# A decoder layer on one core: products of distances 3 and 4 made during attention, three score buffers, eight transposes, moments of the norms on ScalarE

## The chip, the cores and the metric

The kernel runs on one core of a Trainium2 chip, in one launch. The metric is the device time of that launch in microseconds (us), and lower is better. The core has a matrix engine (TensorE, "PE" in the profile, with its weight loads as "PEld"), three engines for work on elements (VectorE "DVE", ScalarE "ACT", GpSimd "POOL") and SyncE ("SP"), which in this kernel issues all the transfers between the device memory and the on-chip memory. TensorE writes into accumulators in PSUM. Each engine takes its instructions strictly in the order of its own queue, and waits on semaphores for what the others produce.

## The reference

The layer has three parts, each followed by a residual sum and a layer norm. There are 16 sequences of 256 tokens with 512 features.

```
x = layernorm(x + attention(x))         # 16 heads of 32, causal, BitLinear weights:
                                        # ternary weights, activations rounded to 8 bits
x = layernorm(x + xattn(ctx, ctx, x))   # 32 heads of 8 features, along the feature axis L = 512
x = layernorm(x + ffn(x))               # rms norm with gamma, BitLinear 512 -> 512
```

The second part is, for each head, with k = v = ctx and q = x:

```
kv  = einsum('bhil,bhjl->bijhl', k_, v_)          # all products of two of the 8 features
y   = causal convolution of kv with ssm_kernel    # along l, 512 taps a head
out = y + kv * D
out = einsum('bijhl,bhil->bjhl', out, q_)
```

Since k and v are the same, kv(i, j) equals kv(j, i), so that 36 of the 64 products are enough. The kernel orders them by the distance d = j - i. With the features wrapped around (feature 8 is feature 0 again) distances 0 to 3 have 8 products each and distance 4 has 4.

## The kernel before

**Attention (first part of the time, up to about 429 us).** The 16 sequences run through a pipeline written out by hand: `step(b)` lists for every engine the stages of sequences b-2 to b+3 in the order in which they are issued, and `last_step` does so for the last three. For each sequence there are four groups of four heads. `scan` makes scores and takes their maxima (L341, L346). `weigh(b, g)` makes the scores again, transposed (L374, L381), takes the exponential on ScalarE into a tile p (L386), zeroes what lies above the diagonal with two selects on GpSimd (L390), and adds two of p's parts into `both` there (L396). `values(b, g)` multiplies p with the values (L409) and sums p and `both` (L416) on TensorE. The tiles p and low come from the pool `hp` with three buffers. Further stages divide by the sums (`divide_sums`, `divide`), round the result (L182, L188), turn it by a transfer (`turn_out`, L473), multiply it with the output weights (`close`, L482), take the norm's statistics (`moments`, `normalize`), and turn the normed rows into x1t (`keep`, L528, L529). `lay` (L355 to L358) splits the maxima for the next sequence. SP's queue holds, in a step, the input rows (L233), the residual rows (L425) and the transfers that transpose (`turn_out` L473, `turn_in` L279).

**The heads (from about 430 us).** 32 heads follow each other. For head h, `load` issues three transfers: the context c (L745), its first four features once more (L746), and the taps w (L749), each into one of three buffers. The products kv, a tile of 576 columns for each of four blocks of 128 positions, are made from c by `square` on ScalarE for distance 0 (L760), and by `multiply(k)` on GpSimd (L754): distance 1, then distance 2 together with distance 4, then distance 3. `copy` brings the head's x1t as q (L772, L773) on ScalarE. `block(lb)` convolves on TensorE: output block lb needs lb + 1 products of a 128 x 128 matrix of taps with kv, in two halves of 288 columns (L785), into a tile y of two PSUM banks, of which there are two buffers. VectorE then multiplies y with q in five operations (L797, L800, L803, L809, L812) into `own` and `turn`. `add` sums on GpSimd: own + turn (L960), and for blocks 1, 2 and 3 (FOLDED) it folds the four parts into two (L962). `read` transposes these parts with TensorE and sums them in PSUM (L820), two transposes for a folded block and four for block 0, so ten for a head, into the tile tok (two buffers). The last head's block 3 is read without adding (`read_all`, L975).

From tok on, the norm and the feed-forward part follow. `second_moments` takes mean and variance on VectorE (L835, L837), and writes a quarter of variance plus epsilon (L840) for one or two forms. `engine_roots` takes the square root on ScalarE (L845), `newton` betters it (L851 on VectorE, L855 on ScalarE), `inverse_roots` inverts (L863). `second_centred` and `second_max` (L878, L882) and the small operations of `second_norm` give the scales; ScalarE makes x2 (L888) and the rounded row (L897, L188), `turn` transposes it by a transfer (L902), `feed_product` multiplies it with the weights on TensorE (L907), `feed_forward` makes r3 (L911) and its statistics on VectorE by the same `moments2`, and `finish` norms it (L926) and stores it (L927). The loop at L1072 gives the order: in its turn h, the blocks of head h stand between the reads and the norm of head h-1, the feed-forward product of head h-2 and the store of head h-3. `last_heads` writes the end out.

Of the kernel before, what the change touches and what calls it, by code (L numbers as in the profile page):

```python
# [15 lines left out]
P = 128  # L16
# [16 lines left out]
def decoder_kernel(ctx: ExitStack, tc: tile.TileContext, x, ctx_t, w_q, w_k, w_v, w_o, ker, d_skip, gamma, w_f, out):  # L33
# [8 lines left out]
    taps = taps_pool.tile([XH, E + P], F32, name="taps")  # L42

# [174 lines left out]
    hp = att.enter_context(tc.tile_pool(name="hp", bufs=3, side="right"))  # L218
# [314 lines left out]

    def on(stage, b, *more):
        if 0 <= b < B:
            stage(batches[b], *more)

    def step(b):


        on(scan, b + 1, 0)
        on(lay_turned, b, b)
        on(fetch_x, b + 3, b + 3)
        on(fetch_again, b - 1, b - 1)
        on(values, b - 1, NB - 1)
        on(begin_batch, b + 2)
        scale = project_qk(batches[b + 2], 0, (0,), wait=True) if b + 2 < B else None
        on(spread, b + 2, b + 2)
        on(save_sums, b - 1)
        on(moments, b - 2)  # L550
        if scale:
            scale()
        on(weigh, b, 0)
        if b < 2:
            weight_round(3 + b, 0)
        if b == 0:
            weight_size(4, nc.scalar)
        on(project_qk, b + 2, 1)
        on(normalize, b - 2)
        on(divide_sums, b - 1)  # L560
        on(divide, b - 1, 0)

        on(scan, b + 1, 1)
        on(divide, b - 1, 1)
        on(out_scales, b - 1)
        on(values, b, 0)
        on(weigh, b, 1)
        if b == 0:
            weight_scale(4, weight_total(ps, 4))
        if b < 2:  # L570
            weight_round(3 + b, 1)
            weight_store(3 + b, 0)
        on(project_qk, b + 2, 2)
        on(out_scaled, b - 1)
        on(keep, b - 2, b - 2)

        on(scan, b + 1, 2)
        on(fetch_scales, b + 3, b + 3)
        on(out_rounded, b - 1)
        on(turn_out, b - 1)  # L580
        on(project_v, b + 2, 0)
        on(values, b, 1)
        on(values_scale, b + 3)
        on(fetch_scaled, b + 3, b + 3)
        on(weigh, b, 2)
        on(project_v, b + 2, 1)
        on(project_qk, b + 2, 0, (1,))
        if b < 2:
            weight_store(3 + b, 1)

        on(scan, b + 1, 3)
        on(project_qk, b + 2, 3)
        on(lay, b + 1, b + 1)
        on(fetch_rounded, b + 3)
        on(turn_in, b + 3, b + 3)
        on(values, b, 2)
        on(weigh, b, 3)
        on(close, b - 1)

    def last_step():  # L600
# [6 lines left out]
        fetch_again(n, B - 2)  # L607
        values(n, NB - 1)
        save_sums(n)
        weigh(m, 1)  # L610
        normalize(k)
# [117 lines left out]
    with ExitStack() as l2:  # L729
        lp = l2.enter_context(tc.tile_pool(name="lp", bufs=3, side="right"))  # L730
        cp = l2.enter_context(tc.tile_pool(name="cp", bufs=2, side="right"))
        ps_y = l2.enter_context(tc.tile_pool(name="ps_y", bufs=2, space=PSUM, side="right"))
        pb = l2.enter_context(tc.tile_pool(name="pb", bufs=1, side="right"))
        gam = pb.tile([P, E], F32, name="gam")
        op = l2.enter_context(tc.tile_pool(name="op", bufs=5, side="right"))
# [5 lines left out]
        def prepare(h):  # L741
# [22 lines left out]
            def multiply(k):  # L764
                part(k * P, XD, 0, k)
                if k == 2:
                    part(4 * P, 4, 0, 4)

# [6 lines left out]
            return w, kv, q, multiply, copy, square  # L775

        FOLDED = (1, 2, 3)
        Y0 = E - HALF

        def products(lb, w, kv):  # L780
            y = ps_y.tile([P, 2 * E], F32, name="y")
# [51 lines left out]
        def moments2(src, roots, forms):  # L833
            st = sm.tile([P, 6], F32, name="st2")
            nc.vector.bn_stats(st, src)  # L835
            mv = sm.tile([P, 2], F32, name="mv2")
            nc.vector.bn_aggr(mv, st)  # L837
            for i in forms:
                a, b = FORMS[i]
                nc.vector.tensor_scalar(roots.quarter[:, i : i + 1], mv[:, 1:2], a / 4, b / 4, ALU.mult, ALU.add)  # L840
            return mv[:, 0:1]
# [23 lines left out]
        def shifted(mean, res):  # L865
            shift = sm.tile([P, 1], F32, name="shift")
            nc.vector.tensor_scalar(shift, mean, res, -1.0, ALU.mult, ALU.mult)
            return shift
# [7 lines left out]
        def second_centred(m):  # L876
            m.xn = fp.tile([P, E], F32, name="xn")
            nc.vector.scalar_tensor_tensor(m.xn, m.flat, m.mean, gam, ALU.subtract, ALU.mult)  # L878
# [65 lines left out]

        def copy(m, *blocks):
            m.inputs[4](*blocks)
# [40 lines left out]
        def last_heads(three):  # L987
# [3 lines left out]
            read(last, 0)  # L991
            read(last, 2)
# [28 lines left out]
        with tc.manual_schedule(engines=by_hand):  # L1021
# [42 lines left out]
            ps_k = l2.enter_context(tc.tile_pool(name="ps_k", bufs=2, space=PSUM))  # L1064
            ps2 = l2.enter_context(tc.tile_pool(name="ps2", bufs=2, space=PSUM))
# [6 lines left out]
            for h in range(XH):  # L1072
# [5 lines left out]
                on(read, h - 1, 0)  # L1078
                on(read, h - 1, 2)
                on(multiply, h + 1, 1)  # L1080
                on(square, h + 1)

                on(block, h, 1)
# [7 lines left out]
                if h > 0:  # L1091
                    newton(roots)
# [3 lines left out]
                on(feed_product, h - 2)  # L1096
                if h > 0:
# [6 lines left out]
                on(copy, h + 1)  # L1104
                on(feed_forward, h - 2, ahead)
# [3 lines left out]
                on(read, h, 1)  # L1109
# [38 lines left out]
```

## Time and profile before

| | us |
|---|---|
| median of three runs | 853.55 (853.28 to 854.99) |
| the profiled execution, whole time | 852.3 |
| the profiled execution, its span | 850.6 |
| busy, share of the span: PE | 793.9 (93%) |
| PEld | 558.9 (66%) |
| DVE | 688.3 (81%) |
| ACT | 426.9 (50%) |
| POOL | 583.5 (69%) |

The span is cut into 40 slices below; each digit is the busy share of a slice in tenths (9 is 90% or more), and PEclk is the clock that TensorE was granted, in tenths.

```profile
PE   4889999999999999998768999999999999999993
PEld 3556666666666666665546777777777777777772
DVE  6757887787897778877556889888988898889885
ACT  6455655656655555664553344344434443344434
POOL 5265454554545545544638999999999999999980
PEclk9999999999999999999989999999999999999997
```

The two parts can be seen in POOL's row: half busy in attention, nearly always busy from slice 23 on. Times that name a moment are us from the start of the span. A row of the timeline gives start, length, engine, line, operation, tiles and shapes, and in brackets the idle time before it with what ended it. A row of the chain of waits gives start, length and what it was; "issue" is time in which nothing is seen to be waited for.

### The profile page before, as it was taken

The numbers are of one execution on the slowest core, as the hardware profiler recorded it, in microseconds if no ns is written. First come the engines' busy times: TensorE is split into PE (matmuls) and PEld (weight loads), VectorE is DVE, ScalarE is ACT, GpSimd is POOL, SyncE is SP. The second block draws the span as 40 slices with busy tenths as digits, with TensorE's granted clock in tenths as the row PEclk, the third lists the DMA queues.
The fourth block names the chain that finished last, engine by engine and source line by source line (L and its number), as shares of the span: only waits on it lengthen the run. The fifth ranks groups of instructions, "written<-read, shape, count | busy, mean of one in ns | idle before, by whom it ended". The sixth has DMA issues, their size and how long they took to land.

```text
span 850.6 us, 20122 instructions
## 1 busy us (share of the span) xinstructions
PE 793.9 (93%) x7678; PEld 558.9 (66%) x7754; DVE 688.3 (81%) x1889; ACT 426.9 (50%) x707; POOL 583.5 (69%) x652
## 2 busy tenths in 40 slices
PE   4889999999999999998768999999999999999993
PEld 3556666666666666665546777777777777777772
DVE  6757887787897778877556889888988898889885
ACT  6455655656655555664553344344434443344434
POOL 5265454554545545544638999999999999999980
PEclk9999999999999999999989999999999999999997
DMA  9112323332222222120240232433233333332311
GB/s 316 51 23 61 70 64 76 76 77 39 51 70 70 76 77 55 42 48 23 66 122 13 76 89 66 94 100 92 69 88 100 94 73 83 99 95 73 81 38 56
DMA packets 102207, 64.51 MB, mean 76 GB/s; under 512 B 66464, under 2 KB 83104, under 8 KB 102112
## 3 DMA queue, kind: packets, MB, share of 16 engines
q1 hardware_dynamic: 102112, 63.23, 28.3%
q8 instruction: 61, 1.00, 0.5%
q14 instruction: 34, 0.28, 0.1%
HBM read 43.34 MB, written 8.47 MB: 61 GB/s over the span
## 4 chain that ended last, share of the span: by engine, by line
PE 80%; DVE 7%; ACT 6%; issue 4%; POOL 3%; DMA 0%; ACTq 0%; POOLq 0%; DVEq 0%
PE y L785 34%; PE s L341 6%; PE acc L293 6%; PE s L381 6%; PE tok L820 5%; ACT p L386 4%; PE pv L409 4%; PE s L334 4%; DVE nmax L346 3%; PE acc_o L482 3%; PE acc_f L907 3%; PE sums L416 2%; PE s L374 2%; PE acc_v L311 2%; PE tp L528 1%
## 5 line engine op out<-in xcount | busy, mean ns | idle before, releaser
L785 PE MATMUL y<-kv,w 128*128 128x288 f32 x1280 | 334.8, 409 | 0.3 <-POOL kv L754 0.3
L785 PEld LDWEIGHTS y<-kv,w 128*128 128x128 f32 x1280 | 236.0, 190 | 60.7 <-POOL kv L754 0.8
L390 POOL TENSOR_SCALAR_AFFINE_SELECT p<-p 128x512 f32<-128x512 f32 x128 | 81.3, 659 | 139.5 <-ACT p L386 129.1
L960 POOL TENSOR_TENSOR own<-own,turn 128x512 f32<-128x512 f32 x127 | 162.0, 1275 | 12.1 <-DVE turn L812 9.9
L754 POOL TENSOR_TENSOR kv<-c 128x512 f32<-128x512 f32 (+1 forms) x128 | 144.4, 1140 | 2.9 <-PE sums L416 2.9
L346 DVE TENSOR_REDUCE nmax<-s 128x4 f32<-128x512 f32 (+1 forms) x128 | 116.5, 952 | 35.4 <-PE s L341 35.4
L386 ACT ACTIVATE p<-s 128x1536 f32<-128x1536 f32 x64 | 92.9, 1452 | 70.3 <-PE s L381 70.2
L396 POOL TENSOR_TENSOR both<-p 128x512 f32<-128x512 f32 x64 | 82.3, 1286 | 5.3
L845 ACT ACTIVATE root<-quarter 128x3 f32<-128x3 f32 (+2 forms) x34 | 7.0, 205 | 150.4 <-DVE quarter L840 150.4
L962 POOL TENSOR_TENSOR own<-own 128x256 f32<-128x256 f32 x95 | 69.1, 727 | 7.4
L797 DVE SCALAR_TENSOR_TENSOR own<-y,q 128x128 f32<-128x128 f32 x128 | 36.7, 286 | 43.7 <-PE y L785 35.7
L293 PE MATMUL acc<-xit,w 128*128 128x256 bf16 x504 | 68.9, 276 | 3.1 <-DVE w L158 2.9
L803 DVE TENSOR_TENSOR turn<-y,q 128x384 f32<-128x384 f32 x128 | 70.2, 548 | 0.0
L800 DVE TENSOR_TENSOR own<-y,q 128x384 f32<-128x384 f32 x128 | 70.1, 548 | 0.0
L293 PEld LDWEIGHTS <-w 128*128 128x128 bf16 x512 | 46.0, 100 | 23.9 <-issue 8.5
L341 PE MATMUL s<-kt,qt 32*128 32x128 f32 (+1 forms) x1024 | 60.0, 348 | 0.0
L820 PE MATMUL tok<-ident,own 128*128 128x128 f32 x318 | 57.7, 283 | 1.7 <-POOL own L962 1.5
L820 PEld LDWEIGHTS tok<-ident,own 128*128 128x128 f32 x318 | 37.8, 141 | 30.0 <-POOL own L962 20.1
L381 PE MATMUL s<-qt,kt 32*128 32x256 f32 (+1 forms) x1024 | 57.4, 335 | 0.0
L409 PE MATMUL pv<-p,va 128*32 128x256 f32 (+1 forms) x1024 | 54.9, 332 | 0.0
L421 ACT COPY ot<-pv 128x256 f32<-128x256 f32 x64 | 23.9, 373 | 50.8 <-PE pv L409 50.2
L334 PE MATMUL s<-mask,ident_h 128*128 128x256 bf16 x256 | 38.3, 272 | 11.1 <-ACT p L386 9.9
(148 smaller groups left out, 1348.4 us busy)
## 6 DMA issues: line engine op xcount, KB each, us to landing
xt<-in_x SPq DMA_DIRECT2D x16, 512.0 KB, 4.6
xr<-in_x SPq DMA_DIRECT2D x16, 512.0 KB, 5.2
c<-in_ctx_t SPq DMA_DIRECT2D x32, 256.0 KB, 3.3
w<-taps SPq DMA_DIRECT2D x32, 256.0 KB, 4.2
out_y<-res SPq DMA_DIRECT2D x31, 256.0 KB, 2.3
c<-in_ctx_t SPq DMA_DIRECT2D x32, 128.0 KB, 3.3
x1t<-in_w_q SPq DMA_DIRECT2D x1, 1024.0 KB, 6.4
x1t<-in_w_k SPq DMA_DIRECT2D x1, 1024.0 KB, 9.7
```

The lines of the kernel that those rows point to most:

```text
L293: nc.tensor.matmul(acc[:, j, :], w[:, c, o * P : (o + 1) * P], m.xit[:, c].rearrange("p t k -> p (t k)"), start=(c == 0), stop=(c == NB - 1),)
L341: nc.tensor.matmul(s[:, r, lo:hi], m.qt[rows, g, q0 : q0 + P], m.kt[rows, g, 0:nk], start=False, stop=True, skip_group_check=True,)
L346: nc.vector.tensor_reduce(m.nmax[:, t, :, g], s[:, :, cols], AX.X, ALU.max, negate=True)
L381: nc.tensor.matmul(s[:, r, lo:hi], m.kt[rows, g, k0 : k0 + P], m.qt[rows, g, q0:S], start=False, stop=True, skip_group_check=True,)
L386: nc.scalar.activation(p, s[:, :, 0 : 3 * P], AF.Exp)
L390: nc.gpsimd.affine_select(out=own, in_=own, compare_op=ALU.is_ge, fill=0.0, base=0, pattern=[[0, 4], [1, P]], channel_multiplier=-1,)
L396: nc.gpsimd.tensor_tensor(both, p[:, :, P : 2 * P], p[:, :, 2 * P : 3 * P], ALU.add)
L409: nc.tensor.matmul(acc[rows, q0:S], m.va[:, j, 4 * g + r, :], p[:, r, src], start=(j == 0), stop=(j == 1), skip_group_check=True, tile_pos ...
L754: nc.gpsimd.tensor_tensor(kv[:, :, at : at + n * B].rearrange("p c (i b) -> p c i b", b=B), c[:, :, i : i + n, :], c[:, :, i + d : i + d + ...
L785: nc.tensor.matmul(y[:, Y0 + k * HALF : Y0 + (k + 1) * HALF], lhs, kv[:, mb, k * HALF : (k + 1) * HALF], start=(mb == 0), stop=(mb == lb),)
L820: nc.tensor.matmul(tok[:, lb, :], lhsT=own[:, d, :], rhs=ident, is_transpose=True, start=(d == last), stop=(d == 0))
L960: nc.gpsimd.tensor_tensor(own[:, 0:4, :], own[:, 0:4, :], turns[lb], ALU.add)
```

## The change

The products of distances 3 and 4 of heads 2 to 30 are made during attention, on GpSimd, from a context tile of their own, and stored in a tensor in device memory (far_d); in the part of the heads a transfer fetches them into kv, and `multiply(3)` does nothing for these heads. The pool hp has two buffers. `multiply` makes distance 4 together with distance 3.

```
+    FAR = P + P // 2
+    far_d = taps_pool.tile([XH, P, NB, FAR], F32, name="far_d")
-    hp = att.enter_context(tc.tile_pool(name="hp", bufs=3, side="right"))
+    hp = att.enter_context(tc.tile_pool(name="hp", bufs=2, side="right"))
+    farp = att.enter_context(tc.tile_pool(name="farp", bufs=1, side="right"))
...
+    far = Far()
+    far.heads = range(2, XH - 1)
+    far.c, far.loaded, far.waiting = [], far.heads.start, []
+
+    def far_load():
+        if far.loaded in far.heads:
+            c = farp.tile([P, NB, XD, B], F32, name=f"far_c{far.loaded % 2}")
+            nc.sync.dma_start(c, ctx_t[far.loaded])
+            far.c.append((far.loaded, c))
+            far.loaded += 1
+
+    def far_multiply():
+        h, c = far.c.pop(0)
+        kv = farp.tile([P, NB, FAR], F32, name="far_kv")
+        for at, n, i, j in ((0, 5, 0, 3), (5 * B, 3, 5, 0), (P, 4, 0, 4)):
+            nc.gpsimd.tensor_tensor(
+                kv[:, :, at : at + n * B].rearrange("p c (i b) -> p c i b", b=B),
+                c[:, :, i : i + n, :], c[:, :, j : j + n, :], ALU.mult,
+            )
+        far.waiting.append((h, kv))
+
+    def far_pass():
+        for h, kv in far.waiting:
+            nc.sync.dma_start(far_d[h], kv)
+        far.waiting = []
+        if len(far.c) < 2:
+            far_load()
```

In `step(b)` a `far_pass()` stands after fetch_again and one after keep (both from b = 1), and a `far_multiply()` after weigh(b, 0) (from b = 2) and one after weigh(b, 2) (from b = 1). In `last_step`:

```
         fetch_again(n, B - 2)
+        far_pass()
+        far_multiply()
+        far_pass()
         values(n, NB - 1)
         save_sums(n)
         weigh(m, 1)
+        far_multiply()
+        far_pass()
         normalize(k)
```

In the part of the heads, block 0 is folded too, so that a head takes eight transposes. y has three buffers of two banks each, in a fixed rotation; for that tok and the feed-forward accumulator have one bank each instead of two.

```
             def multiply(k):
+                if h in far.heads and k == 3:
+                    return
                 part(k * P, XD, 0, k)
-                if k == 2:
+                if k == 3:
                     part(4 * P, 4, 0, 4)
+            def fetch_far():
+                if h in far.heads:
+                    nc.sync.dma_start(kv[:, :, 3 * P : NPAIR], far_d[h])
...
-        FOLDED = (1, 2, 3)
+        FOLDED = (0, 1, 2, 3)
...
-            y = ps_y.tile([P, 2 * E], F32, name="y")
+            place = order.pop(0)
+            y = (ps_z if place == 2 else ps_y).tile([P, 2 * E], F32, name=f"y{place}")
...
-            ps_k = l2.enter_context(tc.tile_pool(name="ps_k", bufs=2, space=PSUM))
-            ps2 = l2.enter_context(tc.tile_pool(name="ps2", bufs=2, space=PSUM))
+            ps_k = l2.enter_context(tc.tile_pool(name="ps_k", bufs=1, space=PSUM))
+            ps2 = l2.enter_context(tc.tile_pool(name="ps2", bufs=1, space=PSUM))
+            ps_z = l2.enter_context(tc.tile_pool(name="ps_z", bufs=1, space=PSUM))
+            order.extend((2, 1, 0) * (2 * XH))
```

Mean and variance of both norms are taken on ScalarE: a copy with accumulation gives the sum, a square with the mean as bias and accumulation gives the variance.

```
         def moments2(src, roots, forms):
-            st = sm.tile([P, 6], F32, name="st2")
-            nc.vector.bn_stats(st, src)
-            mv = sm.tile([P, 2], F32, name="mv2")
-            nc.vector.bn_aggr(mv, st)
+            total = sm.tile([P, 1], F32, name="total2")
+            nc.scalar.activation(unused, src, AF.Copy, accum_out=total)
+            minus_mean = sm.tile([P, 1], F32, name="minus_mean")
+            nc.scalar.activation(minus_mean, total, AF.Copy, scale=-1.0 / E)
+            squares = sm.tile([P, 1], F32, name="squares")
+            nc.scalar.activation(unused, src, AF.Square, bias=minus_mean, accum_out=squares)
             for i in forms:
                 a, b = FORMS[i]
-                nc.vector.tensor_scalar(roots.quarter[:, i : i + 1], mv[:, 1:2], a / 4, b / 4, ALU.mult, ALU.add)
-            return mv[:, 0:1]
+                nc.scalar.activation(
+                    roots.quarter[:, i : i + 1], squares, AF.Copy, scale=a / (4 * E), bias=b / 4
+                )
+            return minus_mean
```

The order of the stages in the loop over the heads:

```
                 on(read, h - 1, 0)
+                on(read, h - 1, 1)
                 on(read, h - 1, 2)
                 on(multiply, h + 1, 1)
                 on(square, h + 1)
+                on(copy, h + 1)
 
+                on(fetch_far, h + 1)
                 on(block, h, 1)
...
                 on(second_centred, h - 1)
+                on(second_max, h - 1)
+
+                on(block, h, 2)
+                on(feed_product, h - 2)
                 if h > 0:
                     newton(roots)
-                on(second_max, h - 1)
-
-                on(block, h, 2)
-                on(feed_product, h - 2)
+                on(feed_forward, h - 2, ahead)
                 if h > 0:
                     inverse_roots(roots)
...
                 on(finish, h - 3, roots, h - 3)
-                on(copy, h + 1)
-                on(feed_forward, h - 2, ahead)
 
                 on(block, h, 3)
                 on(add, h, 2)
-                on(read, h, 1)
             last_heads(ahead)
```

In `last_heads` a read of block 1 is added. The signs of the two places that use the mean follow (minus_mean is added).

More of the change, by code (lines that the diff above doesn't have):

```diff
@@ L532, in keep @@
             )
+    class Far:
+        pass
+    far = Far()
[22 more added lines that the diff above has]
+            far_load()
     def on(stage, b, *more):
@@ L544, in step @@
         on(fetch_again, b - 1, b - 1)
+        if b > 0:
+            far_pass()
         on(values, b - 1, NB - 1)
@@ L553, in step @@
         on(weigh, b, 0)
+        if b > 1:
+            far_multiply()
         if b < 2:
@@ L575, in step @@
         on(keep, b - 2, b - 2)
+        if b > 0:
+            far_pass()
         on(scan, b + 1, 2)
@@ L585, in step @@
         on(weigh, b, 2)
+        if b > 0:
+            far_multiply()
         on(project_v, b + 2, 1)
@@ L607, in last_step @@
         fetch_again(n, B - 2)
+        far_pass()
+        far_multiply()
+        far_pass()
         values(n, NB - 1)
@@ L610, in last_step @@
         weigh(m, 1)
+        far_multiply()
+        far_pass()
         normalize(k)
@@ L731, in decoder_kernel @@
         cp = l2.enter_context(tc.tile_pool(name="cp", bufs=2, side="right"))
-        ps_y = l2.enter_context(tc.tile_pool(name="ps_y", bufs=2, space=PSUM, side="right"))
+        ps_y = l2.enter_context(tc.tile_pool(name="ps_y", bufs=1, space=PSUM, side="right"))
         pb = l2.enter_context(tc.tile_pool(name="pb", bufs=1, side="right"))
         gam = pb.tile([P, E], F32, name="gam")
+        unused = pb.tile([P, E], BF16, name="unused")
         op = l2.enter_context(tc.tile_pool(name="op", bufs=5, side="right"))
@@ L773, in copy @@
                 nc.scalar.copy(q[:, c, XD:EXT, :], x1t[:, h, c, 0 : EXT - XD, :])
-            return w, kv, q, multiply, copy, square
-        FOLDED = (1, 2, 3)
+            return w, kv, q, multiply, copy, square, fetch_far
+        FOLDED = (0, 1, 2, 3)
         Y0 = E - HALF
+        order = [0, 1, 0]
         def products(lb, w, kv):
-            y = ps_y.tile([P, 2 * E], F32, name="y")
+            place = order.pop(0)
+            y = (ps_z if place == 2 else ps_y).tile([P, 2 * E], F32, name=f"y{place}")
             for mb in range(lb + 1):
@@ L866, in shifted @@
             shift = sm.tile([P, 1], F32, name="shift")
-            nc.vector.tensor_scalar(shift, mean, res, -1.0, ALU.mult, ALU.mult)
+            nc.vector.tensor_scalar(shift, mean, res, None, ALU.mult)
             return shift
@@ L877, in second_centred @@
             m.xn = fp.tile([P, E], F32, name="xn")
-            nc.vector.scalar_tensor_tensor(m.xn, m.flat, m.mean, gam, ALU.subtract, ALU.mult)
+            nc.vector.scalar_tensor_tensor(m.xn, m.flat, m.mean, gam, ALU.add, ALU.mult)
         def second_max(m):
@@ L943, in multiply, with fetch_far @@
             m.inputs[3](k)
+        def fetch_far(m):
+            m.inputs[6]()
         def copy(m, *blocks):
@@ L991, in last_heads @@
             read(last, 0)
+            read(last, 1)
             read(last, 2)
@@ L1078, in decoder_kernel @@
                 on(read, h - 1, 0)
+                on(read, h - 1, 1)
                 on(read, h - 1, 2)
@@ L1081, in decoder_kernel @@
                 on(square, h + 1)
+                on(copy, h + 1)
+                on(fetch_far, h + 1)
                 on(block, h, 1)
@@ L1090, in decoder_kernel @@
                 on(second_centred, h - 1)
-                if h > 0:
-                    newton(roots)
                 on(second_max, h - 1)
@@ L1096, in decoder_kernel @@
                 on(feed_product, h - 2)
+                if h > 0:
+                    newton(roots)
+                on(feed_forward, h - 2, ahead)
                 if h > 0:
@@ L1103, in decoder_kernel @@
                 on(finish, h - 3, roots, h - 3)
-                on(copy, h + 1)
-                on(feed_forward, h - 2, ahead)
                 on(block, h, 3)
                 on(add, h, 2)
-                on(read, h, 1)
             last_heads(ahead)
```

## The prediction

> **What bounds the kernel now.** First the busy time by stretch: attention (65 to 429 us) and the heads of the second part (481 to 832 us); columns are stretch, length, then busy time and instructions of TensorE, its weight loads, VectorE, ScalarE, GpSimd, then granted clock and DMA.
>
> ```profile
> 65.00:429.00 364.00, 348.38 (x5338) 236.53 (x5375) 288.39 (x561) 208.63 (x284) 184.80 (x232) 1.00 0.26 62
> 481.00:832.00 351.00, 349.48 (x1540) 257.49 (x1568) 312.77 (x1103) 150.30 (x319) 331.50 (x317) 1.00 0.32 83
> ```
>
> GpSimd is half idle in attention and 94% busy among the heads; ScalarE is 43% busy there. TensorE looks full, so next the chain of waits over one head (start, length, what), where a full engine still shows stalls:
>
> ```profile
> 649.92 0.48 PE y L785 x2
> 650.41 0.22 PE tok L820 x2
> ...
> 654.47 0.39 PE tok L820 x2
> 654.85 2.91 PE y L785 x12
> ...
> 658.63 3.88 PE y L785 x16
> ```
>
> Block 3 of one head ends at 650.40 (call it T), of the next at 662.51: a period of 12.10. Two transposes take 0.22 unhindered; those before block 2 take 0.39. The timeline of all engines says why:
>
> ```profile
> 650.66 0.29 DVE L797 SCALAR_TENSOR_TENSOR own<-y,q 128x128 f32<-128x128 f32 x1
> ...
> 651.92 0.21 DVE L812 TENSOR_TENSOR turn<-y,q 128x64 f32<-128x64 f32 x1
> ...
> 652.28 1.27 POOL L960 TENSOR_TENSOR own<-own,turn 128x512 f32<-128x512 f32 x1 [0.33 <-DVE turn L812]
> ...
> 653.64 0.72 POOL L962 TENSOR_TENSOR own<-own 128x256 f32<-128x256 f32 x1
> ...
> 654.41 0.20 PEld L820 LDWEIGHTS tok<-ident,own 128*128 128x128 f32 x2 [0.40 <-POOL own L962]
> ```
>
> The reader is to see a **ring**: VectorE multiplies block 3's y, GpSimd adds (L960, L962), TensorE waits to transpose the sum, and only then starts block 2, the feed-forward product and the next block 3. Block 2 starts at 654.85 = T+4.45, and 2.91 + 0.86 + 3.88 = 7.65 follow: 12.10. So the period is the ring's, not TensorE's sum.
>
> **The heads after the change.** TensorE's own sum: 40 rows of y at 0.2425 (0.97 for four) = 9.70, feed-forward 0.86, eight transposes at 0.11 = 0.88: 11.44. Now the ring. VectorE started at T+0.26; where it waits for y alone it starts 0.10 after (block 1 ends 654.47, L797 at 654.57). The 0.16 between is the statistics of the other norm (L835, L837, L840), which move to ScalarE. From VectorE's start all stays: L812 ends 1.47 later, GpSimd starts 0.15 after that, its two adds end at +2.08 (652.28 to 654.36), block 2 starts 0.49 later. T + 0.10 + 1.47 + 0.15 + 2.08 + 0.49 = T+4.29, plus 7.65: **a period of 11.94, 0.16 less**. TensorE could be there at T + 0.97 + 0.66 + 1.94 + 0.22 = T+3.79: the two transposes saved, and those moved, only lengthen its wait to 0.50. The 29 periods from the fourth head to the end give 29 x 0.16 = **-4.6**. If VectorE were still busy at T+0.10 this would be 0.
>
> Does anything else take the ring's place?
> - GpSimd a head: four adds of 1.27, four folds of 0.73, two products of 1.28 = 10.6, against 11.8 before; it is done 0.3 after the next T and needed at T+1.72. Covered.
> - VectorE loses two statistics passes (0.69 + 0.18 and quarters) a head. Its last small operation after the new order: block 2 picked up at T+7.30, done 8.77, then inv_root, r3 in 0.9, res at 9.94 behind ScalarE's three L855 (0.94), 1.15 of small ones: free at T+11.1, needed at 12.04.
> - ScalarE: a statistics pass here is a Copy with accumulation 0.63 (like L760), the accumulator read 0.19 (L132's), a small one 0.20 (L845), a Square with a pointer 0.71 (L897) with its read, a small one: 2.0 in a chain; bounds 1.7 and 2.7 (all small ones as L855's 0.377, all large as L926's 0.80). Its head is then some 10 of 11.9 us, and it has 1.7 us of waiting for inv_root left.
> - tok has one buffer: x2 (0.78) must end before the next head's first transpose. L855 ends T+9.9, r3's pass 2.0, x2 ends T+12.7, 0.7 after the next T; TensorE asks at 0.97. By the upper bound 1.3 after, 0.35 late, inside the ring's 0.50. Nothing.
> - y: TensorE comes to block 1 at T+1.63, and VectorE reads block 3 until T+1.57 or later; two buffers would tie here, the third takes the tie away. The moved copies of q start behind res at T+2.6 and wait for that same reading, already over; read 1, moved, is counted in the 3.79.
> - The far products come in by a fourth load a head behind c, c and w in SP's queue, which stands behind the out store, now some 3 us after T: issued by T+5.5, landing by T+10.5 (w: 4.2 us), needed at T+12. Covered by 1.5; without that cover, late one for one.
>
> In the first heads GpSimd sets the pace (449 to 471): head 1's products end 0.63 later because head 0's block 0 is folded (0.73), but head 2 has two products less. The walk ends 0.2 ahead: **-0.2** (bounds -0.8, +0.8).
>
> **Attention.** A head's far products are three GpSimd products of 320, 192 and 256 elements: between the rows of 512 (1276 ns) and 256 (732 ns) 0.87 + 0.60 + 0.73, 2.1 us with the usual overlap; 29 heads, 61 us. In a step GpSimd waits 3.52 us before the second group's selects (225.31) and 3.61 before the fourth's (237.93): each hides one. SP's stores wait for them, and turn_out's transposes stand behind; but those wait for ScalarE until 227.4, the store for 223.9. The third p buffer: exp waits two groups back, which TensorE has done. **0** for the steps; 2 x 2.1 a step if the gaps were gone.
>
> The last step has no gaps. GpSimd's timeline there:
>
> ```profile
> 416.42 1.23 POOL L390 TENSOR_SCALAR_AFFINE_SELECT p<-p 128x512 f32<-128x512 f32 x2
> 417.73 1.28 POOL L396 TENSOR_TENSOR both<-p 128x512 f32<-128x512 f32 x1
> 419.12 1.23 POOL L390 TENSOR_SCALAR_AFFINE_SELECT p<-p 128x512 f32<-128x512 f32 x2
> ...
> 424.87 1.22 POOL L390 TENSOR_SCALAR_AFFINE_SELECT p<-p 128x512 f32<-128x512 f32 x2
> 426.18 1.27 POOL L396 TENSOR_TENSOR both<-p 128x512 f32<-128x512 f32 x1
> ```
>
> Two sets of products go in, after 419.0 and after the next group's sums. The first ends 421.2, the second group's sums 423.8; the second set has to wait until the one far_kv buffer is stored (2.3 to 3.3 us as the 256 KB transfers: 423.6 to 424.7) and ends 426.0 to 426.8. Third group's sums: 428.6 to 429.4, the last 431.2 to 432.0. TensorE does values(2) by 429.4, then the transposes, acc_o and keep, 3.0 to 3.3 us, and values(3) at 432.4 to 433.2 against 429.10. Behind it stand the last batch's division and norm, then the first head: **+3.5** (2.5 to 5).
>
> **The end.** Nothing hides latency there. The chain of waits:
>
> ```profile
> 839.65 0.80 ACT res L926
> 840.45 0.59 ACT fit L196
> ...
> 843.80 0.71 DVE st L835
> 844.53 0.19 DVE mv L837
> 844.75 0.16 DVE quarter L840
> ```
>
> A VectorE pass takes 1.14 to the root (843.78 to 844.93), ScalarE's 2.0. The last head's second norm gets +0.9. Then the pass for the head before it stands in ScalarE's queue ahead of the fit copy, 2.0 where there was nothing. The last pass adds 0.9. **+3.8** (3.0 to 5.0). The Trainium skill speaks against moving such passes (ScalarE: Activation LUTs, Rules for kernel authors: adds and multiplies belong on VectorE). By that rule every pass would be a loss, 64 x 0.9 = 58 us; by the rows ScalarE is idle 4.83 and 1.48 us in a head and the loss shows only where nothing covers it.
>
> **The sum.** -4.6 - 0.2 + 0 + 3.5 + 3.8 = +2.5 on this execution's 852.3 (span 850.6 and 1.7 around it). The median of the runs, 853.55, lies 1.25 above it: **856.0**.
>
> **Rivals.**
> - *The ring opens and TensorE sets the period* (not slower). If the two adds ran shorter once VectorE works less beside them, by the 0.50 of the wait, a head takes 11.44: 856.0 - 29 x 0.50 = **841.5**. For it: VectorE falls from 89% busy by about two us a head. Against: L960 and L962 take 1275 and 728 ns, and the same kind takes 1286 in attention (L396), beside quite other VectorE work. 0.17.
> - *The last step swallows its products*: if the store lands early and close covers the rest, +3.5 falls away: **852.5**. Against: from 412.98 to 427.45 GpSimd rests for about one us in all. 0.18.
> - *The products hinder VectorE in attention* (slower): the second set would run 234.3 to 236.4, and VectorE's L355 to L358 stand at 235.54 to 236.42, with 0.85 spare before L483. L182 takes 0.49 to 0.95 us on VectorE, so such stretching exists. If the four (0.2 each) had to wait for the set's end, they would end at 237.5, 1.1 later than now and 0.25 beyond the spare; with one stretch of 0.46 like L182's half counted, 0.35 a step, x 14 = 5: **861**. The Trainium skill names a cause (GPSIMD Engine Reference, Specifications: shared SBUF interfaces, contention with VectorE instructions of two SBUF inputs or a two-port mode). 0.13.
>
> My forecast has 0.52; its own range, from the terms' bounds, is 852 to 861. Against no change I count 0.2% (1.7 us), about what a measurement tells apart: faster, the first rival and a little of the second, 0.22; within, most of the second and the forecast's lower end, 0.25; slower, 0.53. The range that holds 8 in 10 goes from 847, between first rival and forecast, to 862.
>
> **What would show it.** Right: from block 3's end to the next 11.94, the weight load of the third pair of transposes waiting longer for the fold, VectorE idle before block 3's first product; the last group's sums near 431.5; three statistics passes on ScalarE after the last tok, the fit copy 3 us further behind that tok than now. A period of 11.5 would make the prediction wrong downward, a period above 12.1 or steps of attention over 25.2 us upward.

## The result and the profile after

The changed kernel takes 857.55 us (median of 12 runs, 855.85 to 859.85) against 853.54 (12 runs, 853.13 to 856.65) of the kernel before on the same chip: a ratio of 1.0033 [1.0021, 1.0045], slower by 4.0 us. The profiled execution took 857.54, its span is 855.8; the one of before took 852.3 and 850.6. So the two profiles are 5.2 apart, and the task is to lay these 5.2 out along the span.

Busy time by stretch, as shown of before (stretch, length, busy time and instructions of TensorE, its weight loads, VectorE, ScalarE, GpSimd, then granted clock, DMA share and GB/s):

```profile
65.00:429.00 364.00, 348.96 (x5373) 235.03 (x5365) 296.13 (x560) 207.06 (x281) 241.39 (x317) 1.00 0.40 111
481.00:832.00 351.00, 341.73 (x1524) 253.05 (x1524) 264.98 (x907) 256.75 (x695) 303.44 (x295) 1.00 0.44 115
```

Work went where it was meant to go: among the heads VectorE falls from 312.77 to 264.98 and GpSimd from 331.50 to 303.44, while ScalarE rises from 150.30 to 256.75; in attention GpSimd rises from 184.80 to 241.39. TensorE falls by 8 in the heads. None of this says yet what the time does.

**The heads.** The chain of waits over one head:

```profile
655.65 1.27 POOL own L1025
...
657.01 0.73 POOL own L1027
...
657.78 0.44 PE tok L877 x2
658.22 2.91 PE y L842 x12
661.13 0.86 PE acc_f L969 x4
662.00 4.85 PE y L842 x20
```

It is the ring that the prediction named: GpSimd's sum, its fold, two transposes that waited for it (0.44), block 2, feed-forward product, block 3 (with block 0 of the next head, x20). From one feed-forward product to the next it takes 11.96 in head after head, where it took 12.10; only the last period is longer, 12.66. There GpSimd makes all products of head 31 beside its sums and its four folds, and TensorE's transposes wait for a fold:

```profile
823.78 0.44 PE L877 MATMUL tok<-ident,own 128*128 128x128 f32 x2 [0.86 <-POOL own L1027]
```

Back in the steady heads, block 3's sixteen rows end at 665.88, and VectorE, which was late by 0.16 before, now waits for them (0.77) and starts 0.10 behind:

```profile
665.98 0.29 DVE L854 SCALAR_TENSOR_TENSOR own<-y,q 128x128 f32<-128x128 f32 x1 [0.77 <-PE y L842]
```

**The last step of attention.** GpSimd's timeline:

```profile
419.82 1.28 POOL L399 TENSOR_TENSOR both<-p 128x512 f32<-128x512 f32 x1
421.05 2.11 POOL L555 TENSOR_TENSOR far_kv<-far_c 128x320 f32<-128x320 f32 x3
423.11 1.22 POOL L393 TENSOR_SCALAR_AFFINE_SELECT p<-p 128x512 f32<-128x512 f32 x2
424.42 1.32 POOL L399 TENSOR_TENSOR both<-p 128x512 f32<-128x512 f32 x1
425.93 2.11 POOL L555 TENSOR_TENSOR far_kv<-far_c 128x320 f32<-128x320 f32 x3 [0.19 <-DMA far_d<-far_kv]
...
431.82 1.27 POOL L399 TENSOR_TENSOR both<-p 128x512 f32<-128x512 f32 x1
```

The two sets of products (L555) stand between the selects, the second after a short wait for the store of the first, and the last sums end at 433.09. TensorE takes up the last group's values at 434.39; before, at 429.17.

**The end.** The chain of waits some 10 us before it, in part:

```profile
843.39 0.62 ACT unused L893 x2
844.03 0.21 ACT minus_mean L895
844.27 0.82 ACT unused L897 x2
845.11 0.20 ACT quarter L900
845.32 0.48 ACT fit L198
```

Mean and variance on ScalarE are two passes over the row, each with a read of its accumulator (hence x2), and two small operations, all in a chain: from 843.39 to 845.31 here, and the same again from 848.56 for the last norm. The first of these stands ahead of the fit copy, where before the copy followed at once on the row of L926 (840.45).

**The 5.2, laid out** (the rows add to 5.3 by rounding):

| stretch | before to after | predicted |
|---|---|---|
| start, up to the first exponential (same instructions in both) | +1.8 | not a term |
| steps of attention | +0.3 | 0 |
| last step | +3.1 | +3.5 |
| first heads | +0.2 | -0.2 |
| 28 heads at 11.96 for 12.10 | -3.9 | -4.6, for 29 |
| last head, 12.66 for 12.10 | +0.6 | counted with the 29 |
| end | +3.6 | +3.8 |
| final store | -0.4 | not a term |

The first row is taken from the first exponential, 41.94 before and 43.75 after. In the steps the distance between the two traces falls to 1.59 at step 1 and grows from there to 2.07 at step 14. The last step is taken from values(3) beyond that, the heads from the ends of block 3, and the end from the last block 3's end to the end of the last row's norm (834.03 to 852.53 against 831.90 to 846.83, each on its own trace's clock).

The first row is no part of the change. Its cause can be seen in the traces, in sixteen matmuls that are the same in both, ahead of any changed instruction. TensorE's timeline, before and after:

```profile
18.54 1.92 PE L293 MATMUL acc<-xit,w 128*128 128x256 bf16 x16 [1.48 <-DVE w L158]
```

```profile
12.70 1.89 PE L296 MATMUL acc<-xit,w 128*128 128x256 bf16 x8 [1.53 <-DVE w L160]
...
18.43 3.59 PE L296 MATMUL acc<-xit,w 128*128 128x256 bf16 x16 [1.47 <-DVE w L160]
...
26.98 1.05 PE L296 MATMUL acc<-xit,w 128*128 128x256 bf16 x8
```

The trace's records of TensorE's granted clock begin at 17.0 before and at 22.4 after (the views print a stretch without a record as 1.00). Ahead of that moment eight such matmuls take 1.89, behind it 1.05. The sixteen stand behind it in before and ahead of it in the after.

In the twelve profiles of the experiments the record begins at 21.2 to 24.3, and the first exponential lies 1.2 to 2.7 behind that of before, also in the one whose attention is that of the kernel before (experiment 5: 22.7 and 2.1). So before's profile was an early one, and without this row the change costs 3.4 by the traces and 4.0 by the medians.

### The profile page after: what moved, and what is told of

It reads as the page before. It is cut to its first block, busy times and chain, and to the rows that moved or that the text cites. A ratio compares the mean times of both kernels' runs of the same rounds, so it can differ in the third digit from the quotient of the medians.

```text
span 855.8 us, 20605 instructions
## 1 busy us (share of the span) xinstructions
PE 787.1 (92%) x7690; PEld 552.2 (65%) x7690; DVE 639.2 (75%) x1665; ACT 545.1 (64%) x1123; POOL 609.9 (71%) x713
## 4 chain that ended last, share of the span: by engine, by line
PE 70%; POOL 10%; DVE 8%; ACT 6%; issue 4%; DMA 1%; POOLq 0%; ACTq 0%
PE y L842 27%; PE s L344 6%; PE acc L296 6%; PE s L384 5%; POOL own L1025 5%; PE s L337 4%; PE pv L412 4%; ACT p L389 4%; DVE nmax L349 3%; PE acc_o L485 3%; PE acc_f L969 3%; POOL own L1027 3%; PE tok L877 2%; PE sums L419 2%; PE acc_v L314 2%
## 5 line engine op out<-in xcount | busy, mean ns | idle before, releaser
L842 PE MATMUL y<-kv,w 128*128 128x288 f32 x1280 | 327.8, 407 | 1.4 <-ACT x1t L532 1.1
L842 PEld LDWEIGHTS y<-kv,w 128*128 128x128 f32 x1280 | 238.5, 191 | 64.0 <-ACT x1t L532 1.4
L1027 POOL TENSOR_TENSOR own<-own 128x256 f32<-128x256 f32 x127 | 92.1, 725 | 10.0
L802 POOL TENSOR_TENSOR kv<-c 128x512 f32<-128x512 f32 x70 | 87.5, 1252 | 2.5 <-PE sums L419 2.5
L854 DVE SCALAR_TENSOR_TENSOR own<-y,q 128x128 f32<-128x128 f32 x128 | 36.7, 286 | 58.8 <-PE y L842 53.5
L917 ACT ACTIVATE full<-quarter,root,inv_root 128x1 f32<-128x1 f32 x96 | 30.4, 377 | 75.4 <-DVE inv_root L913 75.4
L555 POOL TENSOR_TENSOR far_kv<-far_c 128x320 f32<-128x320 f32 (+2 forms) x87 | 61.0, 730 | 0.2 <-DMA far_d<-far_kv 0.2
L424 ACT COPY ot<-pv 128x256 f32<-128x256 f32 x64 | 23.9, 373 | 51.0 <-PE pv L412 50.4
L877 PE MATMUL tok<-ident,own 128*128 128x128 f32 x254 | 40.1, 280 | 11.2 <-POOL own L1027 10.4
L337 PE MATMUL s<-mask,ident_h 128*128 128x256 bf16 x256 | 38.6, 273 | 11.4 <-ACT p L389 9.9
```

Of the source, the lines that this page charges most:

```text
L802: nc.gpsimd.tensor_tensor(kv[:, :, at : at + n * B].rearrange("p c (i b) -> p c i b", b=B), c[:, :, i : i + n, :], c[:, :, i + d : i + d + ...
L842: nc.tensor.matmul(y[:, Y0 + k * HALF : Y0 + (k + 1) * HALF], lhs, kv[:, mb, k * HALF : (k + 1) * HALF], start=(mb == 0), stop=(mb == lb),)
L1027: nc.gpsimd.tensor_tensor(own[:, 0:2, :], own[:, 0:2, :], own[:, 2:4, :], ALU.add)
```

## The experiments

Each varies the changed kernel, but for the fifth, which varies the kernel before. Ratios are to the kernel before, run on the same chip beside them (medians 853.62 for 1 to 4, 853.35 for 5 to 8, 854.41 for 9 to 12). Against the changed kernel, 4.0 above its own kernel before, differences are of these distances. The 95% intervals reach 1.0 to 1.9 us to either side, so that a difference of less than 1.5 us between two medians says little by itself; such ones are read from the traces.

### 1. Moments back on VectorE at the end only

```
+            if roots.vector:
+                st = sm.tile([P, 6], F32, name="st2")
+                nc.vector.bn_stats(st, src)
+                mv = sm.tile([P, 2], F32, name="mv2")
+                nc.vector.bn_aggr(mv, st)
...
+            three.vector = one.vector = end.vector = True
```

The flag is set in `last_heads` alone.

> The changed kernel with the statistics of last_heads alone (second norm of the last head, third norm of the last two) taken on VectorE again; the heads before keep ScalarE. Theory (the end is a chain that nothing covers, and the change added 3.8 us to it): about 3.8 us less than the changed kernel, 3 to 4.5, less some 0.2 for a small operation that negates the mean. Rival (the loss lies in the heads or in attention alone): no difference. In the profile the fit copy of the last head comes some 3 us sooner after the last tok.

854.43 (12 runs), 1.0007 [0.9994, 1.0021]: 0.8 above before instead of 4.0, so the end gives back 3.2. The period of the heads stays at 11.96. The chain of this kernel where the after had its last pass:

```profile
848.47 0.70 DVE st L893
...
849.20 0.19 DVE mv L895
...
849.42 0.17 DVE quarter L898
```

The pass takes 1.1 from 848.47 to 849.59, where ScalarE's took 2.0. From the last block 3's end to the end of the last norm it takes 15.28, against 18.50 in the changed kernel and 14.93 before. The end term is shown, in place and, but for 0.4, in size.

### 2. Products one step earlier, none in the last step

```
-        if b > 1:
+        if b > 0:
             far_multiply()
...
-        if b > 0:
-            far_multiply()
+        far_multiply()
...
-        far_multiply()
-        far_pass()
```

> The changed kernel with the far products begun one step sooner (one set in step 0, two in each of steps 1 to 14), so that none is left in the last step. Theory (in the last step GpSimd has no gap, and two sets and the store between them hold values(2) and values(3) back): values(3) comes 3.1 us sooner, the time is 3.1 us less (2 to 4). Rival (the steps of attention pay for the products, wherever they stand): no difference, or slower, since step 0 has the rounding of weights on GpSimd too.

856.99 (10 runs), 1.0039 [1.0026, 1.0051]: 3.4 above before, 0.6 less than with the products, which is within the intervals. The exponentials of the third and fourth group lag those of the kernel before by 1.05 and 2.06 (beyond what the first two groups lag), as much as they do with the products. ScalarE's timeline shows what holds them:

```profile
423.45 1.45 ACT L389 ACTIVATE p<-s 128x1536 f32<-128x1536 f32 x1 [1.15 <-PE sums L419]
...
427.16 1.45 ACT L389 ACTIVATE p<-s 128x1536 f32<-128x1536 f32 x1 [2.00 <-PE sums L419]
```

They wait not for their scores but for TensorE's sums (L419), that is for a p buffer: with two of them the third group's exponential needs values(0) done, and values(0) stands behind weigh(2) in TensorE's queue. So a second cause, hidden behind the first, holds these exponentials as long.

The 0.6 is also held down by something else. In this profile the granted clock falls to 0.5 from 431.1 to 434.5, which it does not do there in the changed kernel's, and the same matmuls take longer, 3.27 for 1.90 in the changed kernel:

```profile
430.72 3.27 PE L485 MATMUL acc_o<-w,oit 128*128 128x512 bf16 x7 [0.35 <-ACT oit L198]
```
With the transposes behind them (0.96 for 0.60) that is 1.7. Counted from the first exponential, values(3) comes 0.6 later than in the changed kernel; without this stretch it would come an estimated 1.1 earlier.

### 3. The last read of a head moved inside block 2

The ring's stall is TensorE's wait ahead of block 2. Here a third of block 2's products is issued before the read of block 3, and the rest after it.

```
+        def opened(m, lb):
+            if lb not in m.y:
+                m.y[lb] = products(lb, *m.inputs[0:2], mbs=(0,))
...
+                on(opened, h, 2)
+                on(read, h - 1, 3)
```

> The changed kernel with one move on TensorE: the transposes of block 3's sum stand after the first two of block 2's six products and not before all of them. Theory (the period of 11.95 is a ring VectorE, GpSimd, TensorE with 0.5 us of waiting on TensorE): TensorE gets there at T+4.54 and waits no more; the period falls to its own sum, 11.44, or to 11.65 where the single tok ties: 29 x 0.3 to 0.5 = 9 to 15 us less. Rival 1 (TensorE is full already, as its busy share says): no difference. Rival 2 (GpSimd or ScalarE sets the period): 0 to 3 us less.

868.62 (4 runs), 1.018 [1.0158, 1.0202]: 15 above before. The period is 12.38. The chain of waits over one head, in part:

```profile
660.10 0.77 ACT x L951
660.91 0.88 PE tok L878 x6
661.79 2.91 PE y L843 x12
...
666.72 0.76 DVE xn L941
...
669.70 0.94 ACT full L918 x3
...
672.48 0.77 ACT x L951
```

That is another ring: the one tok buffer. It cannot be written until x of the head before is made from it, x stands behind the statistics of r3 on ScalarE (1.84), and these behind full. From 660.10 to 672.48 it is 12.38. With the read where the change has it, the four rows of block 2 (0.97) fall out of it, and the same loop takes an estimated 11.4: it lay hidden half a microsecond under the one that sets the period.

### 4. The three edits together

> The three edits together. Theory: their gains stand in different stretches and add up, 3.6 + 3.1 + 9 to 15, so about 838 to 842 us, faster than both kernels. Rival (one gives back what another wins): less than two thirds of the sum.

865.72 (4 runs), 1.0134 [1.0113, 1.0154]: 12.1 above before, with the period of 12.38 of experiment 3. It carries that loss, less about 3 that the other two edits give back, and says nothing more.

### 5. The read moved inside block 2 in the kernel before

> The kernel before with the move of e3 alone (the transposes of block 3's sum after the first two products of block 2). Theory (the ring set its period of 12.10 too): the period falls to GpSimd's own sum, about 11.8: 31 x 0.2 to 0.3 = 6 to 9 us less than before. Rival (TensorE is full): no difference.

853.69 (12 runs), 0.9998 [0.9982, 1.0014]: nothing. In this kernel the statistics are on VectorE and tok has two buffers, so experiment 3's ring cannot be it; yet the period is again 12.10 (but for the first, 11.96). The chain, in part:

```profile
659.25 0.29 DVE own L798
...
665.44 1.23 POOL kv L754
...
666.67 1.24 POOL own L968
...
668.77 0.44 PE tok L821 x2
669.20 2.05 PE y L786 x8
...
671.35 0.29 DVE own L798
```

VectorE's pick of block 1 (its five operations on the block's y), its statistics, GpSimd's sums and one of its products, TensorE, and again the pick of block 1: a loop of 12.10 over three engines that takes over from the one opened.

### 6. Ten transposes again

```
-        FOLDED = (0, 1, 2, 3)
+        FOLDED = (1, 2, 3)
```

> The changed kernel with block 0 not folded, ten transposes a head as before. Theory (TensorE waits 0.5 us a head for the ring): the two transposes, 0.22 us, lie in that wait, the time stays within 1 us of the changed kernel; the first heads may win 0.6. Rival (TensorE sets the period): 29 x 0.22 = 6.4 us more.

856.9 (10 runs), 1.0043 [1.0026, 1.0059]: 3.6 above before, 0.4 below the changed kernel, and a period of 11.96, here in the last head too, where the changed kernel has 12.66. Two transposes more on TensorE, 29 times 0.22 = 6.4 of its work, cost nothing. It also corrects a row of the after. GpSimd's timeline there names TensorE's transposes as what ended its wait ahead of the ring's sum:

```profile
667.61 1.27 POOL L1025 TENSOR_TENSOR own<-own,turn 128x512 f32<-128x512 f32 x1 [1.32 <-PE tok L877]
```

Were that so, eight transposes there instead of six would have lengthened the period. In this run GpSimd's sum starts at 667.32, when the eight are still under way (666.39 to 667.43). VectorE's last row of the block (L869) ends 0.15 ahead of the sum in both, and it is VectorE that counts.

### 7. All moments on VectorE, in the new order

```
-            roots.cols = cols
+            roots.cols, roots.vector = cols, True
```

The branch of `moments2` is that of experiment 1.

> The changed kernel with all statistics on VectorE, its other edits kept. Theory: VectorE is busy at T+0.10 again, the ring takes back 0.1 to 0.16 us a head, 3 to 4.6 us, and the end gains 3.6: within 1.5 us of the changed kernel. Rival A (the passes on ScalarE cost in every head): 20 us or more faster. Rival B (they saved VectorE's whole two us a head): 20 us or more slower.

855.18 (10 runs), 1.0022 [1.0008, 1.0035]: 1.8 above before. The periods alternate between 11.97 and 12.03, 12.00 on average. So with the other edits in place the statistics on ScalarE bring only 0.04 of the 0.14 that a head gained; with them back on VectorE, 0.10 of the gain stays. In 29 heads they bring 1.2, and at the end they cost over 3.

The traces say where the 0.10 comes from. With the statistics on VectorE, this engine works without a gap from its pick of block 1 to its pick of the next block 3 (L854, here at 658.82 and 667.31). So it comes to block 3 late, and the ring closes over two heads: from T to block 1's end, 0.11 to VectorE's pick, VectorE's stretch without a gap, and 11.85 from the pick of block 3 to the next T. Before, that is 4.06 + 0.11 + 8.19 + 11.85 = 24.21, two periods of 12.10; here it is 3.57 + 0.11 + 8.48 + 11.85 = 24.01, two of 12.00. VectorE's own stretch has grown, and the gain is that TensorE ends block 1 0.49 sooner. Of these, 0.22 are the two transposes less (with ten, in experiment 6, block 1 ends at T + 3.79). The other 0.27 go with the order of the stages and with GpSimd's lighter load; no run parts these two.

### 8. Two y buffers

```
-            order.extend((2, 1, 0) * (2 * XH))
+            order.extend((1, 0) * (2 * XH))
```

> The changed kernel with two score buffers in turn instead of three. Theory (block 1 would wait until VectorE has read block 3, T+1.6, which is when TensorE comes, and TensorE's wait of 0.5 covers the rest): within 1 us of the changed kernel. Rival (the third buffer carries the heads): 0.3 us or more a head, 9 us or more slower.

857.46 (10 runs), 1.0038 [1.0024, 1.0052]; 4.1 above before, and 11.96 in nearly every head. The third buffer, for which tok gave up one of its two, is worth nothing here.

### 9. Read inside block 2, and r3's statistics behind x and the rounded row

Experiment 3's ring needs r3's statistics ahead of x on ScalarE. Here they are taken out of `feed_forward` and follow `turn`.

```
                 on(turn, h - 1)
+                on(third_moments, h - 2, ahead)
```

> The changed kernel with the move of e3 and a second one: the statistics of r3 on ScalarE come after x2 and the rounding of the head behind, not before. Theory after e3 (there is a second ring, tok's single buffer: transposes, statistics, VectorE's block 2, inv_root, the three of L917, r3's pass, x2, transposes; 11.39 in the changed kernel and 12.36 in e3, of which r3's pass is 1.84): it falls to some 10.6, both rings are open, TensorE sets the period, 11.44 to 11.6: 29 x 0.35 to 0.5 = 10 to 14.5 us less than the changed kernel. Rival (something else than tok held e3, the transfer of the far products or VectorE's order): the period stays at 12 or more, no gain over the changed kernel.

861.62 (6 runs), 1.0086 [1.0066, 1.0107]: 7.2 above before. Behind the first heads, the first two periods are 11.44 and 11.44: that is TensorE's own sum as the prediction had it. From then on ScalarE's `full` comes every 12.10, and TensorE's periods vary about it (11.4 to 12.6). A part of the chain of waits between two of them, all of it on ScalarE and VectorE:

```profile
640.67 0.95 ACT full L918 x3
...
644.16 0.62 ACT unused L894 x2
...
648.13 0.59 ACT unused L894 x2
...
652.66 0.09 DVE inv_root L914
...
652.77 0.39 ACT full L918
```

The move took the statistics (L894 at 644.16) out of the time in which ScalarE waits for inv_root, and put them into the loop full, x, rounded row, tok's statistics, xn, pick of block 2, inv_root, full. TensorE has no part in this loop; most of its waits between 500 and 830 us are for the far products:

```profile
PE y L843 <- DMA kv<-far_d: 6.3, 12, 0.9
```

(in all, times, longest). Their transfer stands in SP's queue behind the out store, and so behind ScalarE's loop; from issue to landing it takes 4.4 to 5.9 (median 5.0). So the edit made one loop and took the cover off another wait, the one that the prediction had named with 1.5 to spare.

### 10 and 11. The order of the last step, with and without its products

Experiment 2 left two p buffers with values(0) behind weigh(2). Experiment 10 turns that round; 11 does the same and drops the products from the last step, as 2 did.

```
-        weigh(m, 2)
         values(m, 0)
+        weigh(m, 2)
+        values(m, 1)
         weigh(m, 3)
-        values(m, 1)
```

> The changed kernel with one reordering in the last step: values(0) ahead of weigh(2) and values(1) ahead of weigh(3) on TensorE, so that with two p buffers the exponentials do not wait for values that stand behind the next scores. The far products stay in the last step. Theory after e2 (the two p buffers and the far products each hold the last step back by about 3 us, side by side): GpSimd still holds it, 0 to 1 us less than the changed kernel. Rival (the p buffers alone hold it): 2 to 3 us less.

> e10 together with e2: the reordering, and no far products in the last step. Theory: both causes are gone, exp of groups 2 and 3 comes 0 and 0.8 us later than before the change instead of 1.0 and 2.1, values(3) within 1 us of before, the time 2 to 3 us under the changed kernel. Rival (the gap has a third cause, the clock or the transfers): no more than e2 gave, 0.6.

Experiment 10: 858.52 (7 runs), 1.0052 [1.0033, 1.0072], 4.1 above before: no gain. Experiment 11: 855.37 (12 runs), 1.0017 [1.0002, 1.0033], 1.0 above before and some 3 less than the changed kernel. The last group's exponential shows it best. In 10 it lags that of before by 2.0 (beyond the lag of the first two groups), now waiting for its scores (first row); in 11 by 0.5 (second row):

```profile
427.53 1.45 ACT L389 ACTIVATE p<-s 128x1536 f32<-128x1536 f32 x1 [2.11 <-PE s L384]
```

```profile
426.21 1.45 ACT L389 ACTIVATE p<-s 128x1536 f32<-128x1536 f32 x1 [0.99 <-PE s L384]
```

In 10 these scores stand on TensorE behind values(1), whose sums wait for GpSimd, and so for the products. GpSimd's timeline in 11 no longer has the products there, and its last row for attention, the last sums, ends at 430.32 (433.09 in the changed kernel):

```profile
429.06 1.26 POOL L399 TENSOR_TENSOR both<-p 128x512 f32<-128x512 f32 x1
```

Removing either cause alone gives 0 to 0.6 in the medians and leaves the last exponential where it was; removing both gives some 3. So the two stand side by side. The 0 to 0.6 come with a caution: 10's profile, like 2's, has a granted clock of 0.5 in the last step (428.8 to 432.2), and 11's and the changed kernel's have none there.

### 12. The edits of 1, 9 and 11 together

> e9, e11 and e1 together: both rings open, last step in order, statistics of the last heads on VectorE. Theory: 857.5 less 10 to 14.5, less 2 to 3, less 3: 838 to 843 us, 1.2 to 1.8% faster than the kernel before. Rival: the period stays at 11.95 or above, 851 us or more.

854.51 (12 runs), 0.9999 [0.9985, 1.0012]. Behind the first heads come periods of 11.44, 11.44, and then ScalarE's loop of 12.10, as in 9. The end and the last step are given back, the heads' gain is lost to the loop that 9 made.

No version that was run is faster than the kernel before. Two were not tried: 1 and 11 without 9, by the sums here (857.5 less 3.2 and 3.0) an estimated 851, some 2 less than before; and r3's statistics alone on VectorE with the read inside block 2, which would take 1.84 out of experiment 3's loop of 12.38 and the same work out of 9's. Whether the far products' transfer then comes in time stays open.

## Why the prediction was right, by its steps

The forecast was 856.0, slower by 2.5; the median is 857.55, slower by 4.0. Sign and make-up held: a gain among the heads, and two losses, in the last step and at the end, that outweigh it.

- **The heads' ring** was the right bound. T + 0.10 for VectorE's start is seen to the hundredth (665.88 to 665.98), and TensorE's own sum of 11.44 came out in two periods of 9 and 12. A head gains 0.14 instead of 0.16. Over the 29 periods that makes -3.3 for -4.6: 28 bring -3.9, and the last gives back 0.6, for which the prediction had no term (GpSimd's fold of block 0 beside the products of head 31; without that fold, in 6, the period is 11.96). The reason holds for the kernel as it was changed: the statistics leave VectorE, and it starts at T + 0.10. But it isn't the only way there. By experiment 7 the other edits alone would have brought 0.10, since TensorE then ends block 1 sooner; the prediction didn't look at that path.
- **Two transposes fewer, a third y buffer: nothing.** Shown by 6 and 8 for the changed kernel, for the reason given: TensorE waits in the ring anyway. With the statistics on VectorE the two transposes would count, by the sum under 7.
- **Attention's steps: 0.** Measured +0.04 a step from step 1 on, 0.5, and 0.3 with the first step. The gaps that were to hide the products hid them, and the rival in which they hinder VectorE (861) falls.
- **The last step** was sized well, +3.5 for +3.1, by an incomplete mechanism. "The third p buffer: exp waits two groups back, which TensorE has done" is right in the steps and wrong in the last step, where values(0) stands behind weigh(2). That the sum came out all the same is luck: the second cause lies beside the first and not on top of it (2, 10, 11). The rival in which the last step swallows its products (852.5) falls.
- **The end** is +3.6 for +3.8 in the traces; experiment 1 gives back 3.2. The Trainium skill's rule that adds and multiplies belong on VectorE (ScalarE: Activation LUTs, Rules for kernel authors) held at the end, where nothing covers the longer chain (2.0 for 1.1). Taken for the heads too it would mean a loss of 0.9 a pass, and there the passes brought 0.04 a head.
- **The first rival, 841.5:** the ring opening. The change did not open it, since its two adds stayed at 1.27 and 0.73. Opened by hand it ran into three others: tok's buffer (12.38 with the read moved, an estimated 11.4 without), ScalarE's and VectorE's loop (12.10, made by the edit of 9), the transfer of the far products. In the kernel before (5) a fourth of 12.10 was there.
- **The total** is nearer than its terms. Without the start the traces give +3.4 for +2.5: the heads miss by 1.3, the first heads by 0.4 and the steps by 0.3 one way, the last step by 0.4, the end by 0.2 and the final store by 0.4 the other way.
- **The median's offset:** the prediction added 1.25 to this execution's sum for the early profile of before. The start alone was 1.8 later in the after, since the full clock came later.

## What to carry to other kernels

Where the order of stages is written by hand, the period of a loop is its longest ring of waits, and other rings can lie close under it, as here; write out the three or four longest before valuing an edit that opens the first. An operation moved off a busy engine gained here only what it had cost in the ring (0.04 of its 1.1 us, with the other edits in place), and it cost its whole difference where nothing covered it, at the end. When two causes hold the same stage side by side, removing one shows little: read which wait ends last after the edit, and remove both. An edit that was worth nothing in one kernel (the two transposes) can count in the next, when another ring sets the period.

## What the hardware showed unexpectedly

- The records of TensorE's granted clock begin between 17.0 and 24.3 us in the fourteen profiles, in kernels whose matmuls up to there are the same. Ahead of that, eight equal matmuls took 1.89 us, behind it 1.05. Before's record begins first and its first exponential comes first (17.0 and 41.94), that of experiment 1 comes late (23.9 and 44.46). What sets the moment isn't shown.
- Granted clocks of 0.5 for 3.4 or 6.8 us stand between 408 and 435 us in the profiles of 1, 2, 4, 5 and 10, and in none of the others. In 5 such a stretch of 6.8 moved the exponentials behind it by 2.2, in a kernel whose attention is that of before. A comparison of two executions should look for them first.
- A mean and variance over 512 elements takes 2.0 us on ScalarE, with a second instruction of 0.19 after each accumulation to read it, and each step waiting for the one before; VectorE's takes 1.1. Hidden in a wait it was free, and moved by one stage it stood whole in a loop (1.84 of 12.10 in experiment 9, and of 12.38 in 3).
